# Layer 3 of a four-layer convolution kernel: the order in which VectorE masks two pairs of heads, and ScalarE copies them

## Chip, cores and metric

The kernel runs on one core of one Trainium2 chip. The metric is device time in microseconds (us) of one launch; the time of a version is the median of its runs.

## What is computed

The input x is 4 x 256 x 48 x 48 in float32 (batch, channels, rows, columns). Four layers follow one another, each as x + f(groupnorm(x)): a dilated 7x7 attention-weighted convolution (layer 0), a 3x3 convolution with binary weights (layer 1), a 3x3 convolution with ternary weights (layer 2), and a windowed linear attention (layer 3). Only layer 3 is touched here. Cut to what matters, the reference for it is:

```
q = sigmoid(Wq x);  k = sigmoid(Wk x);  v = Wv x, normalised per head
Ik  = integral image of k;   Ikv = integral image of (k outer v)
for w in (1, 2, 4):                 # windows of side 64//w in general, 48//w here
    wk, wkv = box sums of Ik, Ikv over the window round each pixel
    attn = (q . wkv) / (q . wk + 1e-6)
out = Wout concat(attn over w) + bout
```

There are 8 heads of 32 channels. A box sum of k outer v, multiplied by q, is the same as scores q.k over all pixels of the box, times v. That is how the kernel does it: it makes the scores of a block of queries against a tile of keys once, multiplies them by a 0/1 mask for each of the three window sizes, and multiplies the masked scores by v. The half sides of the windows are HALVES = [24, 12, 6].

## The kernel before

**Stages.** Layers 0 to 2 run batch by batch in the first 1429 us. Layer 3 takes the rest. Its queries are cut into blocks of 8 rows (RB = 8, so 6 blocks per image), its keys into tiles of 8 rows by 16 columns (128 keys, one per partition). One block belongs to a batch `b`, a half of the channels `ct` (4 heads) and a row block `rb`; there are 4 x 2 x 6 = 48 blocks. For each block `tiles_of` (L1827) lists the key tiles `(a, c)`: row block `a`, column tile `c` in the order 1, 0, 2.

**Kinds of tiles.** A tile is *near* when `a` is at most one row block from `rb`: all three windows see it (`many`, L1755). A tile two row blocks away lies whole inside the widest window in its rows (`full`, L1753), and the middle window sees part of it. A tile three row blocks away is seen by the widest window alone and not in full. There are 384 near tiles, 192 at distance two and 144 at distance three. Near and far tiles alternate as long as there are both.

**One step of the stream.** The four heads of a block are two pairs. For each tile the program writes, in this order:

1. `scores` (L1694) for the first pair and for the second. TensorE multiplies queries by keys into a PSUM tile `s` of two banks, one bank for each head of the pair. The pool `ps_s` has two buffers, so the first pair always has one and the second pair the other; TensorE writes the next tile's first pair only when every reader of this tile's first pair is done.
2. `masked` (L1712) makes the masked scores in SBUF tiles `sm0` (widest window), `sm1` (middle), `sm2` (narrowest), one set for each pair:
   - `copy` (L1761): ScalarE copies the columns in which the widest mask is all ones into `sm0`; for tiles that are `full`.
   - `middle` (L1757): VectorE multiplies `s` by the middle mask into `sm1`; for near tiles.
   - `widest` (L1767): VectorE multiplies the remaining edge columns of `s` by the widest mask into `sm0`, one or two small pieces; at distance three it does the whole `sm0`.
   - GpSimd multiplies `sm0` by the mask of the narrowest window (near tiles) or of the middle one (distance two), first pair, then second. It reads SBUF only.
3. `sums` (L1805) of the tile two steps earlier (LAG = 2): TensorE multiplies its masked scores by v into three accumulators, windows in the order middle, widest, narrowest. After the last tile of a block ScalarE copies the accumulators to `stage`.
4. `advance` (L254 in `until`, L2005): side jobs take a step each, such as the next batch's projections, the running sums of k (`k_sums`, L1529), the norms (`norms`, L1571) and the end of a block (`finish`, L1868). They put work on all engines.

**What sets the order.** Every instruction goes through `InOrder` (L134), which keeps each engine's instructions in the order in which the program writes them. Between engines the framework makes a wait for each dependence. It also keeps two engines from reading one PSUM bank at the same time: of two readers on different engines, the one that the program writes first goes first, and the other waits for it. So the order of the six calls at L1778 to L1783 sets each queue's order, and, bank by bank, whether VectorE waits for ScalarE or ScalarE for VectorE.

All engine instructions carry one line in the profile, L142, that of the helper in `InOrder`; the groups are told apart by the names of their tiles.

Of the kernel before, what the change touches and what calls it, by code (L numbers as in the profile page):

```python
# [145 lines left out]
def conv_preact_kernel(  # L146
# [1336 lines left out]
    with (  # L1483
# [187 lines left out]
        def rows_seen(wi, a, rb):  # L1671

            h = HALVES[wi]
            return (
                max(0, a * RB - h + 1 - rb * RB),
                min(RB, a * RB + RB + h - rb * RB),
            )

        def cols_seen(wi, c):
            h = HALVES[wi]  # L1680
            return max(0, c * KC - h + (wi > 0)), min(W, c * KC + KC + h)

        class Block:
# [28 lines left out]
            def masked(self, a, c, ss):  # L1712

                rb = self.rb
                all0 = rows_seen(0, a, rb), cols_seen(0, c)
                (r0, r1), (c0, c1) = all0
                wis = [wi for wi in range(NW) if seen(wi, a, rb)]
                pairs = [
                    {
                        wi: smp.tile(  # L1720
                            [P, 2, RB, min(W, KC + 2 * HALVES[wi])],
                            F32,
                            tag=f"sm{wi}",
                            name=f"sm{wi}",
                        )
                        for wi in wis
                    }
                    for _ in ss
                ]

                def view(tiles, wi, rows, cols):
                    (y0, _), (x0, _) = rows_seen(wi, a, rb), cols_seen(wi, c)
                    return tiles[wi][
                        :, :, rows[0] - y0 : rows[1] - y0, cols[0] - x0 : cols[1] - x0
                    ]

                def times_mask(engine, wi, rows, cols, dst, src):
                    mr = rb * RB + rows[0] - (a * RB - HALVES[wi] + 1)
                    mc = cols[0] - (c * KC - MCOL0[wi])
                    nr, ncol = rows[1] - rows[0], cols[1] - cols[0]  # L1740
                    m = mask[wi][:, mr : mr + nr, mc : mc + ncol]
                    engine.tensor_mul(
                        dst, src, m.unsqueeze(1).to_broadcast([P, 2, nr, ncol])
                    )

                def of_banks(s, tiles, wi, rows, cols):
                    src = s[:, :, rows[0] - r0 : rows[1] - r0, cols[0] - c0 : cols[1] - c0]
                    times_mask(dve, wi, rows, cols, view(tiles, wi, rows, cols), src)

                f0, f1 = max(0, c * KC + KC - HALVES[0]), min(W, c * KC + HALVES[0] + 1)
                full = abs(a - rb) * RB + RB <= HALVES[0]  # L1753

                many = seen(NW - 1, a, rb)  # L1755

                def middle(s, tiles):  # L1757
                    if full and many:
                        of_banks(s, tiles, 1, rows_seen(1, a, rb), cols_seen(1, c))

                def copy(s, tiles):  # L1761
                    if full:
                        act.copy(
                            view(tiles, 0, (r0, r1), (f0, f1)), s[:, :, :, f0 - c0 : f1 - c0]
                        )

                def widest(s, tiles):  # L1767
                    if not full:
                        of_banks(s, tiles, 0, *all0)
                        return  # L1770
                    for p0, p1 in ((c0, f0), (f1, c1)):
                        if p0 < p1:
                            of_banks(s, tiles, 0, (r0, r1), (p0, p1))

                first, second = zip(ss, pairs)
                copy(*first)  # L1778
                middle(*second)
                copy(*second)  # L1780
                middle(*first)
                widest(*first)
                widest(*second)  # L1783
                for tiles in pairs:

                    wi = NW - 1 if many else 1
                    if wi in wis:
                        rows, cols = rows_seen(wi, a, rb), cols_seen(wi, c)
                        src = view(tiles, 0, rows, cols)
                        times_mask(pool, wi, rows, cols, view(tiles, wi, rows, cols), src)  # L1790
                return [
                    {wi: view(t, wi, rows_seen(wi, a, rb), cols_seen(wi, c)) for wi in wis}
                    for t in pairs
                ]
# [28 lines left out]
        def seen(wi, a, rb):  # L1823
            r0, r1 = rows_seen(wi, a, rb)
            return r0 < r1
# [226 lines left out]
```

## Time and profile before

| | |
|---|---|
| time, median of 3 runs | 3783.98 us (3771.21 to 3786.39) |
| profiled execution | 3775.4 us, TensorE clock 0.952 |
| layer 3 in it | from 1429 us to the end |

Busy time by engine and stage (us; the mean of TensorE's granted clock in the last column):

| stage | length | TensorE | VectorE | ScalarE | GpSimd | clock |
|---|---|---|---|---|---|---|
| 0 to 1429 | 1429.0 | 1182.6 | 939.2 | 262.4 | 153.9 | 0.92 |
| 1429 to 3775 | 2346.0 | 2082.2 | 1548.0 | 773.9 | 1364.2 | 0.97 |

How to read profile lines: a group line gives the engine, the operation, output<-inputs by the program's tile names, the shapes (partitions x elements), how many there are, then busy time, the mean time of one in ns, and the idle time of the engine just before them with what ended it. A line of the list of waits gives who waited for whom, total us, number of waits, and the longest. A line of the timeline gives the start, the length, the engine, the instruction and how many were merged, and in brackets the idle time before it. PE is TensorE, DVE VectorE, ACT ScalarE, POOL GpSimd. A wait for several engines is put down to the one that came last.

### The profile page before, as it was taken

How to read it: one execution, taken by the hardware profiler on the slowest of the kernel's cores; microseconds unless marked ns; L12 is line 12 of the kernel's file. 1: busy time of each engine (PE TensorE's matmuls, PEld its weight loads, DVE VectorE, ACT ScalarE, POOL GpSimd, SP SyncE). 2: the span in 40 equal slices, each digit the busy share in tenths (PEclk: the TensorE clock that was granted, in tenths of full speed). 3: DMA queues.
4: the chain of work that ended last, by engine and by line, in shares of the span. 5: the costliest groups of instructions: out<-in, count | busy, mean ns of one | idle time of the engine just before them, and what ended most of it. 6: DMA issues, size and time to landing. Idle time of an engine off the chain costs nothing. (4 is left out here: it accounts for less than half of the span.)

```text
span 3775.4 us, 68847 instructions
## 1 busy us (share of the span) xinstructions
PE 3264.8 (86%) x26498; PEld 1879.4 (50%) x26498; DVE 2487.2 (66%) x5119; ACT 1036.2 (27%) x2025; POOL 1518.1 (40%) x2184
## 2 busy tenths in 40 slices
PE   3688898998996788988889889899899899989998
PEld 2467686786784564433334334344443344444443
DVE  7876587587583366777666567756577766556665
ACT  0012111111113322433222333332344332233331
POOL 0000120020020034778765486755365766344332
PEclk9798999999997899999999899999999999999999
DMA  7745323324324313345434243533223444101122
GB/s 250 238 135 170 100 104 116 109 95 125 109 75 124 102 70 108 125 136 159 125 103 131 90 136 122 164 97 108 78 95 123 139 116 116 47 31 53 41 60 60
DMA packets 373019, 423.04 MB, mean 112 GB/s; under 512 B 129076, under 2 KB 328532, under 8 KB 371540
## 3 DMA queue, kind: packets, MB, share of 16 engines
q1 hardware_dynamic: 371491, 416.32, 35.6%
q8 instruction: 211, 3.46, 0.4%
q0 software_dynamic: 144, 1.52, 0.2%
q14 instruction: 117, 0.95, 0.1%
q10 hardware_dynamic: 1056, 0.79, 0.1%
HBM read 288.79 MB, written 131.25 MB: 111 GB/s over the span
## 5 line engine op out<-in xcount | busy, mean ns | idle before, releaser
L142 DVE TENSOR_TENSOR sm<-s,masks 128x112 f32<-128x112 f32 (+10 forms) x2592 | 1135.8, 493 | 765.5 <-PE s L142 321.1
L142 POOL TENSOR_TENSOR sm<-sm,masks 128x432 f32<-128x432 f32 (+14 forms) x1152 | 853.3, 755 | 936.5 <-ACT sm L142 672.0
L142 PE MATMUL s<-qs,ks 32*128 32x320 f32 (+3 forms) x5760 | 832.5, 500 | 200.1 <-DVE sm L142 151.2
L142 ACT COPY sm<-s 128x528 f32<-128x528 f32 (+2 forms) x1152 | 594.9, 535 | 1470.7 <-PE s L142 1169.9
L142 PE MATMUL acc<-sm,vs 128*32 128x384 f32 (+18 forms) x13440 | 880.5, 385 | 16.1 <-POOL sm L142 15.8
L142 PEld LDWEIGHTS s<-qs,ks 32*128 32x128 f32 x5760 | 374.1, 185 | 604.7 <-DVE sm L142 232.8
L142 PE MATMUL cv<-vx,wt 128*128 128x288 f32 x2080 | 559.3, 425 | 90.7 <-DVE vx L142 49.1
L142 PEld LDWEIGHTS acc<-sm,vs 128*32 128x32 f32 x13440 | 355.2, 110 | 551.3 <-issue 348.6
L142 PEld LDWEIGHTS cv<-vx,wt 128*128 128x128 f32 x2080 | 402.4, 198 | 212.4 <-issue 53.6
L142 POOL MEMSET v<- 128x16 f32 (+1 forms) x120 | 18.6, 215 | 725.7 <-DVE vx L142 635.7
L142 PE MATMUL cv<-v,wl 128*128 128x384 f32 x1152 | 224.5, 354 | 24.4 <-DVE x L142 9.2
L142 PEld LDWEIGHTS cv<-v,wl 128*128 128x128 f32 x1152 | 214.8, 195 | 34.6 <-issue 16.1
L142 POOL TENSOR_TENSOR pt<-pt 128x144 f32<-128x144 f32 x336 | 187.4, 558 | 22.8 <-DVE pt L142 0.5
L142 POOL TENSOR_TENSOR v<-l2v,v 128x384 fp32r<-128x384 f32 x96 | 109.2, 1168 | 130.2 <-ACT v L142 121.4
L142 POOL TENSOR_TENSOR nhi<-nhi,nq 128x384 f32<-128x384 f32 x144 | 148.3, 1058 | 0.0
L142 PE MATMUL cv<-pad,wl 128*128 128x384 bf16 x864 | 143.1, 327 | 0.0
L142 PE MATMUL out_ps<-o,wout_sb 128*128 128x384 f32 x288 | 122.8, 509 | 9.4 <-DVE o L142 5.4
L142 PE MATMUL out_ps<-stage,wout_sb 128*128 128x384 f32 x288 | 117.3, 489 | 0.4 <-DVE stage L142 0.4
L142 PE MATMUL proj_ps<-wv_sb,xn 128*128 128x256 f32 x288 | 89.5, 438 | 32.3 <-ACT vt L142 19.1
L142 DVE TENSOR_TENSOR vx<-v 128x868 f32<-128x868 f32 x112 | 115.4, 1056 | 0.5
L142 PE MATMUL ap<-seen,xT 120*128 120x120 f32 (+3 forms) x832 | 113.5, 293 | 0.0
L142 PEld LDWEIGHTS <-wl 128*128 128x128 bf16 x864 | 83.8, 97 | 59.1 <-issue 0.4
(162 smaller groups left out, 2859.0 us busy)
## 6 DMA issues: line engine op xcount, KB each, us to landing
wt<-wt SPq DMA_DIRECT2D x48, 768.0 KB
kb_d<-pt SPq DMA_DIRECT2D x48, 576.0 KB
rc<-r_d SPq DMA_DIRECT2D x192, 144.0 KB
nhi<-kb_d SPq DMA_DIRECT2D x120, 192.0 KB
nlo<-kb_d SPq DMA_DIRECT2D x88, 192.0 KB
o_d<-stage SPq DMA_DIRECT2D x24, 576.0 KB
o<-o_d SPq DMA_DIRECT2D x24, 576.0 KB
wl<-wl_d SPq DMA_DIRECT2D x16, 768.0 KB
```

Source lines behind the costliest of these rows:

```text
L142: return lambda *args, **kwargs: self.tc.keep_in_program_order(op(*args, **kwargs))
```

## The change

The calls in `masked` change places. Before, VectorE's middle masks took the second pair first, while ScalarE copied the first pair; then the two engines changed pairs. After, both engines take the first pair ahead of the second: ScalarE's copy of a pair comes first on that pair's banks, then VectorE's middle mask, then the edge pieces. It is for having one order for both engines, in which ScalarE's copies do not stand behind VectorE's masks.

```diff
                 first, second = zip(ss, pairs)
                 copy(*first)
-                middle(*second)
                 copy(*second)
                 middle(*first)
+                middle(*second)
                 widest(*first)
                 widest(*second)
                 for tiles in pairs:
```

Nothing else is changed: the same instructions with the same operands, and ScalarE's and GpSimd's own orders are as before.

## Prediction

> **What bounds the kernel now.** I read the page first (busy shares), then the busy time by stage, then the groups kept apart by shape for VectorE and ScalarE, then the list of waits, and last the timeline of single tiles. The change lies in layer 3 alone, so its window is read apart from the rest.
>
> ```profile
> PE 3264.8 (86%) x26498; PEld 1879.4 (50%) x26498; DVE 2487.2 (66%) x5119; ACT 1036.2 (27%) x2025; POOL 1518.1 (40%) x2184
> ```
>
> ```profile
> 1429.00:3775.00 2346.00, 2082.19 (x20666) 943.65 (x20666) 1548.04 (x3296) 773.85 (x1537) 1364.18 (x1886) 0.97 0.34 103
> ```
>
> The second fence is layer 3 (from 1429 us on; columns: length, busy us of TensorE, weight loads, VectorE, ScalarE, GpSimd, then clock and DMA): 2346 us long; TensorE busy 2082 us, VectorE 1548, ScalarE 774, GpSimd 1364. So TensorE is idle some 260 us there, and those are the only microseconds that a reordering can give or take. The list of waits says what ends them, and how VectorE and ScalarE wait for each other:
>
> ```profile
> DVE sm L142 <- PE s L142: 321.1, 342, 9.2
> ...
> ACT sm L142 <- DVE sm L142: 235.9, 349, 3.8
> ...
> PE s L142 <- DVE sm L142: 151.2, 243, 3.9
> ...
> PE acc L142 <- POOL sm L142: 15.8, 17, 3.3
> ```
>
> Columns: total us, times, longest. More than half of TensorE's idle time, 151 us, ends when VectorE releases a score buffer. GpSimd's small pieces cost TensorE 16 us. ScalarE stands 236 us behind VectorE, in 349 waits for 384 tiles of the kind that is changed. The groups by shape show the masks and copies that change places (the last figures are idle time before them and what ended it):
>
> ```profile
> L142 DVE TENSOR_TENSOR sm<-s,masks 128x624 f32<-128x624 f32 x256 | 194.9, 802 | 98.3 <-PE s L142 94.2 <-ACT sm L142 3.2 <-POOL sm L142 0.8
> L142 DVE TENSOR_TENSOR sm<-s,masks 128x448 f32<-128x448 f32 x256 | 147.9, 619 | 89.0 <-PE s L142 87.6 <-ACT sm L142 0.8
> ...
> L142 DVE TENSOR_TENSOR sm<-s,masks 128x432 f32<-128x432 f32 x256 | 143.7, 602 | 92.8 <-PE s L142 85.2 <-POOL pt L142 3.6 <-POOL sm L142 3.1
> ```
>
> ```profile
> L142 ACT COPY sm<-s 128x528 f32<-128x528 f32 x384 | 229.1, 615 | 489.0 <-PE s L142 382.4 <-DVE sm L142 79.6 <-POOL sm L142 21.6
> ```
>
> The 256 + 256 + 256 masks are the `middle` ones, two in each of 384 near tiles (columns c = 1, 0, 2). Before the first of the two VectorE waits for TensorE's second pair of scores (94.2 + 87.6 + 85.2 = 267 us), and almost never for ScalarE. One near tile (c = 1) in the timeline:
>
> ```profile
> 2511.87 1.56 PE L142 MATMUL s<-qs,ks 32*128 32x384 f32 x8 [0.28 <-DVE sm L142]
> ...
> 2512.88 0.61 ACT L142 COPY sm<-s 128x528 f32<-128x528 f32 x1 [2.07 <-PE s L142]
> ...
> 2513.48 2.28 DVE L142 TENSOR_TENSOR sm<-s,masks 128x624 f32<-128x624 f32 x6 [1.02 <-PE s L142]
> ...
> 2514.38 0.61 ACT L142 COPY sm<-s 128x528 f32<-128x528 f32 x1 [0.88 <-DVE sm L142]
> ...
> 2515.52 1.29 PE L142 MATMUL s<-qs,ks 32*128 32x384 f32 x8 [0.87 <-DVE sm L142]
> ```
>
> Scores of both pairs; ScalarE copies the first pair; 0.60 us after that copy began, the second pair is there and VectorE starts on it, not waiting for ScalarE; ScalarE's second copy starts only when VectorE's first mask has ended. TensorE then stands 0.87 us for the buffers. The near tile's path is: second scores ready, two middle masks, the edge piece(s) of the first pair, next tile's first scores.
>
> **What the Trainium skill says.** PSUM — Partial Sum Buffer, section "PSUM bank collisions raise a hardware error": accesses of two engines to one bank and partition quadrant must be kept apart by semaphores, ScalarE's read against VectorE's read included, whatever the columns. The trace agrees that the program does so: in near tiles the second copy starts 34 to 90 ns after VectorE's mask of that pair ends; in the tiles two row blocks away, which have copies and edges only, the edge starts 32 ns (median) after the copy of its pair ends. TensorE: Matmul & The Clock Gate, opening table of specifications: VectorE's and ScalarE's queues are strict FIFO, so a wait at the head holds all that is behind it. VectorE: DVE Perf Modes, section "Why PSUM operands drop a tier": an fp32 operand in PSUM runs at the plain rate. The rows above agree (624 elements in 802 ns, 448 in 619: 183 ns for 176 elements), and order does not touch it, so every mask and copy keeps its duration.
>
> **The change part by part.** Nothing is added or removed: VectorE's queue goes from second, first, edges to first, second, edges; ScalarE's order and GpSimd's stay. What changes is which engine comes first on a bank, and so three waits.
>
> *Removed:* the second copy's wait for VectorE. ScalarE's 236 us of standing behind VectorE go, and the second copy ends earlier: on average by about 0.70 us, counted tile by tile in the trace (its start now, against the later of the end of the first copy and the second scores). Who gains: GpSimd's small piece of the second pair. But TensorE uses that piece two tiles later (LAG = 2), and its waits on it (16 us in all, 13 pile-ups) come after lumps of other GpSimd work: in each, the first piece had started 3.5 to 10 us after its copy. I take 5 us of gain; bounds 0 and 16.
>
> *Added, first:* the first mask (now of pair 1) waits for ScalarE's copy of pair 1. Behind it in VectorE's queue are the other mask and all edges, and for those TensorE waits. New start = copy start + copy duration + 0.03 us; old start = second scores ready. The tile above: 2512.88 + 0.61 + 0.03 = 2513.52 against 2513.48, 0.04 later. Another (c = 2):
>
> ```profile
> 2189.25 0.48 ACT L142 COPY sm<-s 128x384 f32<-128x384 f32 x1 [2.08 <-PE s L142]
> 2189.33 1.78 DVE L142 TENSOR_TENSOR sm<-s,masks 128x432 f32<-128x432 f32 x4 [0.64 <-PE s L142]
> ```
>
> 2189.25 + 0.48 + 0.03 = 2189.76 against 2189.33: 0.43 later. A third, with c = 0, begins its copy at 2183.23 (0.51 long) and its masks at 2183.76: 0.01 later. Over all 384 near tiles the masks now start 0.44 us (mean) after the first copy starts, and the copy takes 0.53, so 0.13 on the mean. ScalarE's lateness counts in full now: in 67 tiles the copy starts under 0.2 us before the mask. Where the present distance is over 0.6 us (111 tiles), little is gained in return: VectorE is still busy with earlier work there, or the second scores are late.
>
> *Added, second:* the second mask waits for the second copy, so it starts no earlier than second scores + 0.48 to 0.62 + 0.03 us. The first mask takes 0.60 to 0.80, so this bites little, but it takes away most of the gain of an early first mask. With both waits and VectorE's previous work in the count, the second mask ends later by 0.18 us on the mean: 384 x 0.18 = 70 us of later VectorE.
>
> *What of it is on the path:* only where TensorE starts the next tile's scores as soon as the edges end. In the trace that start comes within 0.15 us of the end of the first pair's last edge in 209 of 384 near tiles; in the others TensorE is still on sums, projections or norms. Over those 209 the shift has a mean of 0.21 us, 44 us in sum. Charging every tile's shift against its own distance gives 39 us.
>
> *What takes some of it back:* TensorE's waits on GpSimd (16 us) and on GpSimd's norm products are for work that does not wait for the score buffers; a TensorE that comes later waits less there. I take 8 us of the 39 as absorbed; bounds 0 and 20. Sum: +39 - 8 - 5 = +26 us, 3784 + 26 = 3810 us (0.7%).
>
> **The rivals.**
> *Absorbed* (about 3789): VectorE is late but has 66% duty in the stage, and 175 of 384 tiles have distance to spare. If also half of the 39 us goes into other waits and 15 us come back from GpSimd, 39 - 20 - 15 = +4 to 5 us remain. Against it: 209 tiles have no distance, and the loop scores, masks, scores passes a delay straight on.
> *Faster* (about 3757): the freed ScalarE feeds GpSimd 0.7 us sooner; GpSimd's lateness also stalls VectorE before its masks (33 us on sm, 23 on nhi, 11 on pt) and TensorE (16), 83 us in all. If a third of that goes, and the later masks are absorbed, 3784 - 28 = 3756, with rounding 3757. For it: 1364 us of GpSimd in 2346, and bursts that last. Against it: those bursts are several us long, an earlier piece of 0.7 us does not remove them, and only near tiles' second pieces come earlier.
> *Full pass-through* (about 3840): the shift counts also where other work was the limit today, with more of ScalarE's lateness (stage copies, sigmoids, norm copies) before VectorE: 3784 + 56, being 80% of 70 us.
>
> **How the numbers follow.** Chances: forecast of 3810 0.55, full pass-through 0.07, absorbed 0.25, faster 0.13. Over 0.5% means beyond 3803 or below 3765: slower 0.62, same 0.25, faster 0.13. The range 3770 to 3834 holds the forecast with both bounds of its terms, the absorbed case, and the near part of the faster one; full pass-through and a real gain stay outside.
>
> **What would show it.** Right: the wait of ScalarE's copies for VectorE falls from 236 us to nearly nothing, a wait of the middle masks for ScalarE appears in place of most of the 267 us on TensorE, and TensorE's wait for VectorE before scores grows from 151 us by 25 to 45 us; durations and counts stay. GpSimd's second pieces start earlier without a shorter stage. Wrong: VectorE's masks do not wait for the copies, or TensorE's wait for VectorE stays at 151 us, or the waits on GpSimd fall by more than 20 us.

## The result, and the profile after

The changed kernel takes 3836.15 us (3835.28 to 3855.11, 4 runs) against 3785.18 us (3771.21 to 3788.22, 4 runs) for the one before. These are medians, 51 us apart; the ratio of the means is 1.0154, 95% interval 1.0114 to 1.0194, about 58 us (43 to 73), and this figure is used below. The direction was forecast, the size was not: 3810 us was the forecast and 3834 us the upper end of the range.

The page, the layer 3 window and the waits of the changed kernel, in the columns of the prediction:

```profile
PE 3292.0 (86%) x26498; PEld 1896.7 (49%) x26498; DVE 2468.9 (64%) x5119; ACT 1017.2 (27%) x2025; POOL 1497.7 (39%) x2184
```

```profile
1429.00:3834.00 2405.00, 2115.26 (x20656) 967.25 (x20656) 1526.29 (x3282) 753.52 (x1534) 1341.93 (x1884) 0.96 0.33 99
```

```profile
DVE sm L142 <- ACT sm L142: 620.0, 529, 9.0
...
PE s L142 <- DVE sm L142: 195.8, 268, 3.6
ACT sm L142 <- POOL sm L142: 140.9, 67, 6.8
...
DVE sm L142 <- PE s L142: 58.6, 32, 5.0
...
PE acc L142 <- POOL sm L142: 10.6, 15, 2.6
```

Both windows begin at 1429 us, and this one is 59 us longer. Counted from its own first score matmul (at 1429.5 us before, at 1422.3 after) layer 3 is 66 us longer in these two traces, so it carries all of the difference. VectorE's waits have changed hands: 59 us for scores in place of 321, and 620 for ScalarE in place of 267. ScalarE's 236 us behind VectorE are gone from the list. TensorE's wait before scores grew by 45 us, and its waits for GpSimd's pieces fell by 5. One line was not forecast: TensorE itself is *busy* 33 us longer, with the same instructions, and the granted clock in the window went from 0.97 to 0.96.

The middle masks by shape (254 of the first shape, as the window begins after the first tile):

```profile
L142 DVE TENSOR_TENSOR sm<-s,masks 128x624 f32<-128x624 f32 x254 | 193.7, 803 | 132.9 <-ACT sm L142 132.5
L142 DVE TENSOR_TENSOR sm<-s,masks 128x448 f32<-128x448 f32 x256 | 150.6, 620 | 114.4 <-ACT sm L142 113.7
L142 DVE TENSOR_TENSOR sm<-s,masks 128x432 f32<-128x432 f32 x256 | 146.9, 604 | 113.1 <-ACT sm L142 109.9
```

Their durations stand (803, 620, 604 ns); the wait ahead of them now ends with ScalarE and is 80 us longer in sum (360 us against 280). The same near tile that the prediction read first, in the timeline of the changed kernel:

```profile
2539.16 1.56 PE L142 MATMUL s<-qs,ks 32*128 32x384 f32 x8 [0.28 <-DVE sm L142]
2540.13 1.27 ACT L142 COPY sm<-s 128x528 f32<-128x528 f32 x2 [2.02 <-PE s L142]
...
2540.77 2.28 DVE L142 TENSOR_TENSOR sm<-s,masks 128x624 f32<-128x624 f32 x6 [1.01 <-ACT sm L142]
...
2542.82 1.30 PE L142 MATMUL s<-qs,ks 32*128 32x384 f32 x8 [0.87 <-DVE sm L142]
```

Both copies now run on end, and the masks start 0.64 us after the first copy's start: 0.04 later than before, as worked out for this tile. A tile further on shows the part that was missed:

```profile
2769.18 1.12 ACT L142 COPY sm<-s 128x528 f32<-128x528 f32 x2 [2.56 <-PE s L142]
...
2769.83 2.28 DVE L142 TENSOR_TENSOR sm<-s,masks 128x624 f32<-128x624 f32 x6
...
2771.87 1.20 PE L142 MATMUL s<-qs,ks 32*128 32x320 f32 x8 [1.52 <-DVE sm L142]
...
2774.10 2.65 PE L142 MATMUL proj_ps<-xn,wk_sb 128*128 128x384 f32 x4
```

TensorE stands 1.52 us for VectorE; then four projection matmuls take 2.65 us, where the four of the same form at 2766.67 took 1.56. The windows of this stretch say why (the sixth figure after the length, the one below or at 1, is the granted clock):

```profile
2769.00:2772.50 3.50, 1.98 (x34) 1.29 (x32) 3.50 (x10) 1.51 (x3) 1.37 (x2) 1.00 0.44 169
2772.70:2776.00 3.30, 3.30 (x15) 1.38 (x12) 2.94 (x6) 0.91 (x2) 2.57 (x4) 0.53 0.00 0
```

In the 3.5 us with the wait TensorE was busy 1.98; in the next it ran at half clock. Over layer 3, counted from the clock records of the two traces, time at half clock went from 126 to 193 us.

I counted both traces by tile of the stream (the period of a tile runs from its first score matmul to the next tile's). "Bound" are the 209 near tiles of the prediction whose successor's scores started within 0.15 us of the first pair's last edge before the change. Sums in us:

| | tiles | period, after less before | time without a matmul, before to after |
|---|---|---|---|
| near, bound | 209 | +56.6 | 139.0 to 181.5 |
| near, with distance | 175 | +6.9 | 25.3 to 20.9 |
| two or three row blocks away | 336 | +2.6 | 95.5 to 88.4 |

In sum layer 3 is 66 us longer in these two traces: 31 us more without a matmul, 35 us more with one running. The first is close to the prediction's 26; the second is not in it at all. A second cut of the same tiles separates the two costs: the 650 that ran at full clock in both traces are 35 us longer together, and all of the added standing lies in them; the 70 touched by half clock in either trace are 31 us longer, without standing any longer than before.

### The profile page after: what moved, and what is told of

Read it like the earlier page. It is cut to its first block, busy times and chain, and to the rows that moved or that the text cites. A ratio compares the mean times of both kernels' runs of the same rounds, so it can differ in the third digit from the quotient of the medians.

```text
span 3834.3 us, 68781 instructions
## 1 busy us (share of the span) xinstructions
PE 3292.0 (86%) x26498; PEld 1896.7 (49%) x26498; DVE 2468.9 (64%) x5119; ACT 1017.2 (27%) x2025; POOL 1497.7 (39%) x2184
## 3 DMA queue, kind: packets, MB, share of 16 engines
q0 software_dynamic: 144, 1.52, 0.2%
## 5 line engine op out<-in xcount | busy, mean ns | idle before, releaser
L142 POOL TENSOR_TENSOR sm<-sm,masks 128x432 f32<-128x432 f32 (+14 forms) x1152 | 843.8, 753 | 1011.7 <-ACT sm L142 675.9
L142 PE MATMUL s<-qs,ks 32*128 32x320 f32 (+3 forms) x5760 | 853.5, 507 | 243.6 <-DVE sm L142 195.8
L142 ACT COPY sm<-s 128x528 f32<-128x528 f32 (+2 forms) x1152 | 572.6, 535 | 1523.7 <-PE s L142 1236.4
L142 PE MATMUL acc<-sm,vs 128*32 128x384 f32 (+18 forms) x13440 | 892.3, 390 | 10.8 <-POOL sm L142 10.6
L142 PEld LDWEIGHTS s<-qs,ks 32*128 32x128 f32 x5760 | 393.3, 189 | 646.8 <-issue 301.1
L142 DVE SCALAR_TENSOR_TENSOR x<-cv,alpha,x 128x384 f32<-128x384 f32 x144 | 84.0, 610 | 43.2 <-PE cv L142 42.9
```

What stands on the lines that cost most here:

```text
L142: return lambda *args, **kwargs: self.tc.keep_in_program_order(op(*args, **kwargs))
```

## The experiments

**Theory A:** VectorE's later masks cost what was counted, on the tiles without distance alone, and the longer waits also drop TensorE to half clock, which makes up the rest. **Theory B:** all of VectorE's lateness (70 us) passes on, and the clock is incidental. **Theory C:** GpSimd's backlog, by way of the buffers that ScalarE's copies wait for, now reaches VectorE. All times below are medians; the ratios, and the differences worked out from them, compare means with those of the kernel before in runs on the same chip.

**Filler against the half clock.** Both kernels got matmuls of zeros in the places where TensorE stands longest:

```diff
+                if n < len(stream) and not last:
+                    j, ja, jc, _, _ = stream[n]
+                    if jc == 1 and seen(NW - 1, ja, order[j][2]):
+                        for _ in range(3):
+                            pe.matmul(
+                                blocks[i].accs[0], zeros[:, 0:P], zeros, start=False, stop=False
+                            )
                 if last:
                     done(i)
             advance()
```

> The kernel before, with three matmuls of zeros (128x384, bf16, 0.25 us each by the zero matmuls of the trace) added onto the first accumulator after the sums that follow the scores of each near tile with c = 1, where TensorE stands about 0.8 us today. It keeps TensorE busy through the wait and adds zero to the result. Theory A (the change costs the later masks on the tiles without distance, 39 us, and on top about 30 us because longer waits drop TensorE to half clock): half-clock time falls by some tens of us; the time lies between -20 and +20 us of before, since about a quarter of these tiles have no wait and pay 0.75 us each. Theory B (all of VectorE's lateness passes on, the clock is incidental): +15 to +25 us, the clock's share has no effect.

> The changed kernel with the same filler. Theory A: slower than the kernel before with filler by 35 to 45 us only, and its half-clock time is close to that one's. Theory B: slower than it by the same 51 to 58 us as without filler. Theory C (GpSimd's lateness reaches VectorE through ScalarE's copies, which wait for buffers): 51 to 58 us too.

Measured: the kernel before with filler 3783.25 us, ratio 1.0022 (1.0009 to 1.0036); the changed kernel with filler 3824.22 us, ratio 1.0131 (1.0115 to 1.0147). Between the two lie 41 us where 58 lay without filler. Half clock in layer 3: 108 us and 121 us. TensorE's wait before scores, first the kernel before with filler, then the changed one with it:

```profile
PE s L142 <- DVE sm L142: 110.0, 244, 4.0
```

```profile
PE s L142 <- DVE sm L142: 154.6, 275, 4.0
```

The wait still grows by the same 45 us that it grew without filler, so the filler did not hide the difference in VectorE's lateness; what went is the difference in clock. It is not a clean switch: it costs the kernel before 0.2%, since some of these tiles have no wait to fill. This speaks for A, against B and C, but the times alone do not decide it: with their intervals the 58 us are 43 to 73 and the 41 are about 33 to 49.

**A delay of VectorE alone.** A small instruction between the middle masks, the order of before:

```diff
                 copy(*second)
+                if full and many:
+                    dve.tensor_scalar(spare, spare, 1.0, 0.0, ALU.mult, ALU.add)
                 middle(*first)
```

> The order of before, with one small VectorE instruction (128x2, about 0.17 us by the like rows) between the two middle masks of each near tile: VectorE is late by 0.10 to 0.17 us per near tile, and no wait changes. Theory A: +20 to +35 us of waiting on the tiles without distance, half-clock time up by 20 to 50 us, together +30 to +55 us. Theory B: 384 tiles x the delay, +40 to +65 us, with near tiles that have distance to spare lengthened as much as the others. Theory C: the delay alone is absorbed, +0 to +20 us.

Measured: 3876.95 us, ratio 1.027 (1.0255 to 1.0285), far over what any theory gave, because the delay was mis-sized: the two masks of a near tile now start 0.91 us apart instead of 0.62, so it is 0.29 us and not 0.10 to 0.17. With that size A's own term is 209 x 0.29 = 61 us and B's is 384 x 0.29 = 112. The tiles at full clock in both traces are 63 us longer, the tiles with half clock in either 47 us; half clock went from 126 to 234 us. Near tiles with distance grew by 19 us, bound ones by 80, where B had them grow alike. C's forecast failed: a delay that touches no copy's wait on GpSimd is not absorbed. To separate A from B, the same delay with the filler:

> The small VectorE instruction between the two middle masks (measured: it sets the masks of a near tile 0.29 us further apart, and cost 100 us) together with the filler matmuls of zeros. Theory A: of the 100 us some 60 are lateness on the tiles without distance (209 x 0.29) and the rest mostly half clock, so against the kernel before with filler it is slower by 65 to 80 us only. Theory B (all lateness passes on, 384 x 0.29 = 112 us, the clock is incidental): slower than that by the same 95 to 105 us.

Measured: 3859.28 us, ratio 1.0206 (1.0184 to 1.0227), and so, with the filler's own 1.0022 taken out, about 70 us over the kernel before with filler, where the delay without filler had cost 102 (27 thousandths of 3781). This drop is clear of noise: 96 to 108 us against about 60 to 79. Half clock in layer 3: 149 us. The filler hid nothing of the delay itself: it adds 63 us of standing to the bound tiles with filler and 66 without. A's forecast held.

The two pairs can be put together. Write the lengthening of layer 3 as S + a x (more half clock). From the traces the change gives 66.1 = S + 67.2a without filler and 42.5 = S + 13.5a with it: a = 0.44, S = 37. The delay gives 110.0 = D + 108.0a and 81.5 = D + 40.9a: a = 0.42, D = 64. A microsecond at half clock costs 0.42 to 0.44 us in both, and the rest, 37 and 64, is near what the count on bound tiles says (39 and 61). Each of these is one trace, so the agreement to a few us is worth no more than that.

The runs give the same price without a filler. The kernel before was run 40 times beside these experiments, and each run lists its mean granted clock; the time at half clock is 2 x (1 - clock) x span. Runs with more of it took longer, by 0.41 us for each us (standard error 0.04, correlation 0.87). This is a correlation, as longer waits could bring both, and the four runs of the changed kernel are too few to repeat it. On the mean the changed kernel's four runs have 419 us of half clock in the whole kernel and these 40 have 375. That is 44 us more, not the 67 of the two traces, as the profiled execution before had less half clock than most. At 0.41 it makes 18 us of the 58, about what the filler took away.

**Is it the buffers?** One more buffer for `sm0` in the changed kernel:

```diff
                             tag=f"sm{wi}",
                             name=f"sm{wi}",
+                            bufs=2 * (LAG + 1) + (wi == 0),
```

> The changed kernel with seven instead of six buffers for the masked scores of the widest window (sm0), which ScalarE's copies write and GpSimd reads. In the changed kernel ScalarE waits 141 us for GpSimd to leave these buffers, before the change 40 us. Theory C: this wait, which now stands ahead of VectorE's first mask, is a good part of the loss: 15 to 40 us faster than the changed kernel. Theory A: the wait shrinks and the time stays within 10 us of the changed kernel's (1.0154 times before).

Measured: 3841.36 us, ratio 1.0155 (1.0123 to 1.0188): the changed kernel's time. But its waits, read in the trace of this run, say that the edit did not do what it was for:

```profile
DVE sm L142 <- ACT sm L142: 624.7, 523, 10.4
ACT sm L142 <- POOL sm L142: 200.4, 139, 11.3
PE s L142 <- DVE sm L142: 199.4, 261, 4.4
```

ScalarE's wait put down to GpSimd did not shrink; it grew from 141 to 200 us. So a seventh buffer brings nothing, but this run does not test C. The traces of the two kernels do: if GpSimd held the first copies back more than before, they would start later after their scores. They start 0.17 us after the end of the first pair's score matmuls on the mean of the near tiles, before and after. The added wait on GpSimd is not one that delays VectorE's first mask.

**Half the tiles.** The order of the change where the condition holds, that of before elsewhere; the second run has `c != 1`:

```diff
                 copy(*first)
-                middle(*second)
-                copy(*second)
-                middle(*first)
+                if c == 1:
+                    copy(*second)
+                    middle(*first)
+                    middle(*second)
+                else:
+                    middle(*second)
+                    copy(*second)
+                    middle(*first)
```

> The change in the 128 near tiles with c = 1 alone (the longest copy, 0.62 us), the order of before in the other 256. By the same count as in the prediction, 23 to 27 us of the shift lies in these tiles. Theory A: +23 to +27 us and about 10 us of half clock, +30 to +40. Theory B (every tile counts alike by its shift, 0.27 x 128): +35.

> The change in the 256 near tiles with c = 0 and 2 alone. The count puts 16 to 17 us of shift on tiles without distance. Theory A: +16 to +28 us with half clock. Theory B (0.15 x 128 + 0.12 x 128): +35. If the change's cost were a matter of crossing a threshold in waiting only, one of the two halves would cost nearly nothing.

Measured: 3809.18 us, ratio 1.0075 (1.005 to 1.0099), and 3808.67 us, ratio 1.0079 (1.0051 to 1.0106): 28 and 30 us, which add up to the whole change's 58. The first is 2 us under A's range, the second 2 over, and B's 35 lies within both intervals, so these runs do not separate A from B. There is no single threshold that one half alone crosses. Half clock in layer 3 was 169 and 159 us, so both halves bring some.

**The first wait without the second.**

```diff
                 copy(*first)
-                middle(*second)
-                copy(*second)
                 middle(*first)
+                middle(*second)
+                copy(*second)
```

> The order copy of the first pair, mask of the first, mask of the second, copy of the second: the first added wait (first mask behind first copy) without the second (the second mask waits for no copy), and ScalarE's second copy stays behind VectorE. Theory A: the first wait carries the loss, +35 to +60 us. If the second wait carried it: -5 to +15 us. Theory C: with ScalarE's second copy late again as before, GpSimd's backlog is like before, +10 to +25 us.

Measured: 3966.06 us, ratio 1.051 (1.0493 to 1.0528), 193 us, a miss for all. The count by tile shows that the edit brought a wait of its own: the first pair's last edge ends 1.61 us after the first mask starts (1.64 in the changed kernel), but the second pair's edges stand behind the late second copy and end after 2.33 us (1.98). Far tiles, which the change had left alone, grew by 85 us, and half clock reached 310 us. The wait for the second pair's buffer can be seen in far tiles at full clock: their eight score matmuls take 1.25 us together (1.00 before), and the fifth, the second pair's first, starts 0.30 us after the fourth (0.19 before). The profile counts this as busy, as the records of these matmuls overlap. The run cannot tell the two added waits apart. It shows that the second pair's buffer is on the path too.

**Orders that might beat both.** With VectorE first on both pairs:

```diff
-                copy(*first)
-                middle(*second)
-                copy(*second)
                 middle(*first)
+                copy(*first)
+                middle(*second)
+                copy(*second)
                 widest(*first)
                 widest(*second)
```

> Both pairs with VectorE first on their banks: mask of the first, copy of the first, mask of the second, copy of the second, then the edges. VectorE starts on the first scores instead of the second ones (0.44 us sooner on the mean), and waits for no copy until the second pair's edge. The first pair's buffer comes free about 0.4 us sooner than before, the second pair's 0.1 to 0.2 us sooner. Theory A (what counts is when VectorE's masks start and end, and the half clock that longer waits bring): faster than before by 30 to 60 us, half-clock time lower. Theory C (GpSimd, which now gets its pieces about 0.6 us later, sets the pace through buffers): slower than before by 10 to 40 us.

Measured: 3801.83 us, ratio 1.0048 (1.003 to 1.0066). A's forecast of 30 to 60 us faster was wrong, and the time, about 18 us slower, lies in C's range. Bound near tiles are 41 us shorter, as meant; near tiles with distance are 21 us longer and far tiles 49. VectorE's edges, in this run's trace, tell where (mean ns, then idle time before and what ended it):

```profile
L142 DVE TENSOR_TENSOR sm<-s,masks 128x256 f32<-128x256 f32 x384 | 160.2, 422 | 86.3 <-ACT sm L142 71.9
L142 DVE TENSOR_TENSOR sm<-s,masks 128x240 f32<-128x240 f32 x384 | 155.6, 407 | 135.4 <-ACT sm L142 115.4
```

Before, ScalarE ended 79.4 us of the first group's wait and 105.7 of the second's, all ahead of tiles two row blocks away; in near tiles no edge had idle time ahead of it. Now near tiles' first edges have 83 us of it over all shapes. They wait for copies that stand behind the masks, and the second pair's buffer is released 0.06 us later than before. The next run puts the second pair's edge ahead of its copy, in near tiles (`many`) alone:

```diff
+                if many:
+                    middle(*first)
+                    copy(*first)
+                    middle(*second)
+                    widest(*second)
+                    copy(*second)
+                    widest(*first)
```

> In near tiles: mask of the first, copy of the first, mask of the second, edge of the second, copy of the second, edge of the first; far tiles as before. In the version with VectorE first on both pairs near tiles got shorter, but the tiles after them longer by about as much, and the second pair's edge ended 0.06 us later than before, behind a copy. If that late release of the second pair's buffer is what lengthened the far tiles, they go back to their length here, near tiles gain less, and the time is -15 to +10 us of before. If it was GpSimd's later pieces, which are as late here, the far tiles stay long: +15 to +30 us.

Measured: 3801.4 us, ratio 1.0043 (1.0025 to 1.0061). The far tiles are back at their length (4 us shorter in sum), so it was the late release that had lengthened them. But near tiles gain nothing now (bound +6 us, with distance +33), and the time, 16 us slower, is over the 10 us that was expected and in the range given for GpSimd's later pieces, though not in the tiles where these were to show; half clock in layer 3 was 176 us against 126 before. The last order, again in near tiles alone:

```diff
+                if many:
+                    middle(*first)
+                    copy(*second)
+                    middle(*second)
+                    copy(*first)
+                    widest(*first)
+                    widest(*second)
```

> In near tiles the interleaving of before with the pairs exchanged: VectorE masks the first pair while ScalarE copies the second, then they change; far tiles as before. VectorE starts on the first scores, 0.44 us sooner, but its second mask waits for the second pair's copy, about 0.35 us. Theory A: both buffers come free about 0.1 us sooner than before, 0 to 25 us faster. If only the start of the first mask mattered: 40 us or more faster. Theory C: GpSimd's first piece comes about 1 us later, 10 to 30 us slower.

Measured: 3811.38 us, ratio 1.008 (1.0055 to 1.0104). The masks of a near tile start 0.97 us apart (0.62 before), as the second waits for its copy, and the first pair's edges end 0.07 us later after the tile's first score instead of 0.1 sooner; half clock is 156 us. The gain that was hoped for was lost in that wait. GpSimd's first piece came about 0.8 us later too, the 30 us are within C's range, and its share was not separated. So C fails for the change itself, but for these three orders GpSimd's part stays open. None of the three beats the kernel before.

## Why the prediction was right or wrong

**Where VectorE starts: right.** The two added waits were forecast to end the second mask 0.18 us later on the mean. From the start of the first copy to the end of the first pair's edges it is 2.25 us now and was 2.07: 0.18. The masks start 0.61 us after the copy starts (0.44 before), 0.17 later where 0.13 was worked out.

**What of it is on the path: right.** The shift on the 209 bound tiles was put at 44 us, and 39 went into the sum. TensorE's time without a matmul before scores rose from 200 to 244 us, and the near tiles with distance grew by 7 us only. The full pass-through that the rival of 3840 us supposed did not happen; that its time was nearly measured is luck.

**What takes some of it back: seen in the waits, not in the time.** TensorE's other idle time fell by 13 us (accumulator sums 16 to 11, projections 24 to 16), which is the 8 and 5 that were taken. But the projections' waits end with ScalarE and not with GpSimd, those before norm products did not fall (10 to 11), and the stage did not get the 13 us back. The tiles at full clock in both traces are 35 us longer and the fit gives 37, nearer to the 39 before these terms than to the 26 after them. Some of the idle time may only have moved: at full clock the eight score matmuls of a far tile take 1.05 us where they took 1.00, which counts as busy.

**The sum: wrong, by a term that it lacks.** The step that failed is "TensorE is idle some 260 us there, and those are the only microseconds that a reordering can give or take", and with it the sum "+39 - 8 - 5 = +26 us", which holds only time in which TensorE stands. The runs show a second cost of standing: TensorE then runs at half clock for 3.41 us or a multiple, and its busy time, taken as fixed, grows. The clock was in the page and in every window that was read (0.97 for layer 3), and was charged nothing. In the two traces 67 us more at half clock go with 35 us more of TensorE busy; at 0.43 us each they are 29 us, and 6 are not attributed. In the runs the term is smaller, 17 us of the 58 by the filler and 18 by the clock of the runs. With 18 the forecast of 26 would have been 44, near the lower end of what was measured; without the 13 us taken back it would have been 57. All the signs that were to show the prediction right came: ScalarE's wait for VectorE went, the masks wait for ScalarE, and TensorE's wait for VectorE grew by 45 us. None of them looks at the clock.

The Trainium skill has the mechanism (TensorE: Matmul & The Clock Gate, section "What's actually happening"): a monitor of TensorE's activity passes half of the clock pulses after about 3.4 us idle. The trace agrees on the two states and on the 3.41 us, and differs on what is needed, as the last section shows.

**The rivals.** Absorption failed since 209 tiles have nothing to absorb with. The faster case failed as argued: freeing ScalarE gave GpSimd's second pieces an earlier start (their distance from the first mask fell from 2.04 to 1.36 us), and TensorE's waits for GpSimd's pieces fell by 5 us only.

**What stays open:** the two added waits were not separated by a run; the middle masks' wait for ScalarE is seen, but how much of it is the second copy's rests on the count alone. Why the 13 us did not come back was not tested. And the filler is indirect: it shows that the loss shrinks with the half clock, not what a chip without that clock gate would do.

## What to carry to other kernels

When two engines read the same PSUM banks, the order in the program decides which of them pays for the other's lateness; keep waits away from the engine on whose last read the buffer's release hangs, and follow every buffer to its last reader, not only the first one. When a change lengthens short waits of TensorE in a loop, price the clock as well as the wait: look at the granted clock by window, and count how many windows of 3.4 us are near half busy before it. Busy time is not fixed when waits change.

## What was not expected of the hardware

Waits far shorter than 3.4 us bring half clock. I divided layer 3 into the 3.41 us windows on which the clock records begin, and took each window at full clock, up to the last score matmul, by TensorE's busy share in it, with the clock of the next:

| busy share of the window | before: windows, next at half clock | after: windows, next at half clock |
|---|---|---|
| under 0.50 | 16, 15 | 19, 17 |
| 0.50 to 0.65 | 17, 3 | 38, 15 |
| 0.65 to 0.70 | 12, 1 | 40, 0 |
| over 0.70 | 600, 0 | 548, 0 |

Under half busy the next window is nearly always at half clock, over 0.70 never in these two traces; one wait of 1.5 us together with the small ones round it is enough (the window ahead of the half clock shown above was busy to 0.55). Of the 52 stretches at half clock in both traces 46 have no gap between matmuls as long as 3.41 us at the window ahead of them, so the skill's idle window of about 3.4 us, read as one wholly idle, is not needed here, and the measurement decides. Windows under 0.65 are 33 before and 57 after. The borders are rough, as the busy share is from matmuls whose ends are modelled and can hide waits: in the trace of the first wait without the second, half clock followed 9 of 548 windows over 0.70 too.

A 128x2 instruction of VectorE, meant to take about 0.17 us, put the masks on either side 0.29 us further apart (0.62 to 0.91): consecutive masks start some 0.08 us before the one ahead has ended, and the small instruction is recorded with 0.35 us there (median), where those of its size in the trace before took 0.16 to 0.17.
